# A two-layer decoder on one core: less work for GpSimd in a normalisation, another buffer for the sorted tiles' results, and another order

## The chip, the cores and the metric

The kernel runs on 1 core of one Trainium2 chip. The metric is the device time of one execution in microseconds. TensorE (PE; PEld is its weight load), VectorE (DVE), ScalarE (ACT), GpSimd (POOL) and SyncE (SP) each work through a queue of their own in the order in which the program was built; semaphores join them.

## The reference, cut to what matters

Sixteen sequences of 128 tokens with 256 features go through two decoder layers in float32. Every sub-layer is added to x after a normalisation of x:

```python
def _layernorm(x, axis=-1, eps=1e-05):
    m = jnp.mean(x, axis=axis, keepdims=True)
    v = jnp.var(x, axis=axis, keepdims=True)
    return (x - m) / jnp.sqrt(v + eps)
...
x = x + _L0_attn_ref(_layernorm(x), qk, ov)                    # causal, one head
x = x + _L0_xattn_ref(_layernorm(x), ctx, ctx, mask, ...)      # 16 heads of 16, over the context
x = x + _L0_ffn_ref(_layernorm(x), ...)                        # 16 blocks of 64, the best 4 by a router
x = x + _L1_attn_ref(_layernorm(x), ...)                       # 16 heads, and adds its own input
x = x + _L1_xattn_ref(_layernorm(x), ctx, ctx, cell, ...)      # windows of 64, rotary, four more norms
x = x + _L1_ffn_ref(_layernorm(x), ...)                        # 8 experts of 128, the best 2, and a shared one
```

The last one, for each token t, with `combine` zero for all but two of the eight experts e:

```python
hmid = jax.nn.silu(g) * u            # g, u = x @ w_gate[e].T, x @ w_up[e].T
y = jnp.einsum('tei,ehi->teh', hmid, w_down)
routed_out = jnp.einsum('te,teh->th', combine, y)
out = routed_out + shared_out
```

## The kernel before, in words

**Tiles.** Two sequences make a lane: x[l] is a tile of 128 tokens by 2 by 256, and eight lanes (NL) stay in the on-chip memory from start to end. Matrices are float32; masks, router choices and one-hot products are bfloat16.

**The order.** Every piece of work is a generator (a thread). A planner, the class `Turns`, holds an estimated free time for each engine, a cost for each instruction and a list of free buffers for each tag (`LIMITS`). At each `yield` a thread names the engine that it needs next and the buffers that it takes; `run` picks the thread that could start first by the estimate, ties by rank, and records its instructions up to the next `yield`. The recorded order is the order of every engine's queue on the chip; nothing is reordered there. `LEAD` prefers threads that take score banks (`s`), `RELEASE` is added to the time at which a buffer is given back, and `indexed` (L162) adds 2000 ns to the planned landing of a transfer by index. None of these numbers is an instruction; they act through the order alone.

**Lanes in flight.** `TURN` (L1422) is the list of lane and layer pairs in the order in which they begin, first six lanes of layer 0, then layer 1 of lane 0, layer 0 of lane 6 and so on. At most five are in flight.

**Layer 0** of a lane (`layer_0`): causal attention, attention over the context, block feed-forward; TensorE's groups are pj, pr, s, oT, hp (hidden) and y.

**Layer 1** of a lane (`layer_1`): self attention, windowed attention (which normalises four times: the context, x twice, the heads' output), then, for lanes 0 to 4, `routing`. An attention of one sequence computes its scores twice: once for the maximum (VectorE, `top`), and again with the maximum subtracted inside the product (GpSimd adds it to the queries, `qs`, and spreads the keys, `kb`).

**The experts.** Lanes 0 to 4 are sorted: `routing` scatters each normalised token to two rows of a table in device memory (`to_experts`, 20 transfers by index on GpSimd's queue). When all five are through, `plan` counts the tiles and 27 `expert_tile` threads each gather an expert's weights and 128 tokens (`we`, two transfers by index), multiply, and store 128 results to `by_experts` from ScalarE's queue. One buffer `p` of 1024 columns holds the weights in 768 and the tokens in 256; the results (`yo`) are copied over the tokens. After all tiles and the five `shared` threads, `combining` gathers 20 times from `by_experts` (`yg`) and adds to x. Lanes 5 to 7 are dense: `expert_ffn` computes all eight experts (gu, wb, y) with weights that are loaded after layer 0.

**The normalisation.** `normalise` (L392) has VectorE compute mean and variance (bn_stats and bn_aggr, `mv`). GpSimd then makes `rstd` in two instructions (add, power) and `less` = -mean x rstd in two more. One half of the tile is normalised by VectorE (`xn`, subtract and multiply), the other by ScalarE with `less` as bias and `rstd` as scale. It is called 77 times. GpSimd's instructions on 128 x 2 elements, the indexed transfers (L168) and everything else of GpSimd stand in one queue.

The class of routers (`ranks`, `chosen`): VectorE compares the scores (eq, gt), GpSimd combines them, VectorE counts, and TensorE transposes the choice (`ptt`).

Of the kernel before, what the change touches and what calls it, by code (L numbers as in the profile page):

```python
# [9 lines left out]
F32 = mybir.dt.float32  # L10
# [4 lines left out]
ALU = mybir.AluOpType  # L15
AX = mybir.AxisListType

B, S, D = 16, 128, 256
P = 128
# [62 lines left out]
class Turns:  # L82
# [3 lines left out]

    LEAD = 200.0
    HOP = 70.0  # L90
    HOP_FROM_PE = 200.0
    SWITCH = 91.0
    PART = 0.0
    RELEASE = 0.0

    def __init__(self, nc, limits):
        self.nc = nc
# [64 lines left out]
    def indexed(self, out, out_index, src, src_index):  # L162

        at = lambda i: None if i is None else bass.IndirectOffsetOnAxis(ap=i, axis=0)
        self.charge(POOL, 1050.0)
        self.moved(4 * int(np.prod((src if src_index is None else out).shape)))
        self.now.at += 2000.0
        self.nc.gpsimd.indirect_dma_start(out, at(out_index), src, at(src_index))  # L168

    def fetch(self, out, src):  # L170
# [102 lines left out]
def decoder(ctx: ExitStack, tc: tile.TileContext, a: dict, out: bass.AP):  # L273
# [118 lines left out]
    def normalise(src, free=False):  # L392

        yield DVE
        mv = small.tile([P, G, 2], F32, tag="mv", name="mv")
        for j in range(G):
            st = small.tile([P, 6], F32, tag="st", name="st")
            q.dve("bn_stats", st, src[:, j, :])
            q.dve("bn_aggr", mv[:, j, :], st)
        yield POOL  # L400
        rstd = small.tile([P, G], F32, tag="rstd", name="rstd")
        q.pool("tensor_scalar", rstd, mv[:, :, 1], EPS, None, ALU.add)
        q.pool("tensor_tensor", rstd, rstd, power, ALU.pow)

        less = small.tile([P, G], F32, tag="less", name="less")
        q.pool("tensor_tensor", less, mv[:, :, 0], rstd, ALU.mult)
        q.pool("tensor_scalar", less, less, -1.0, None, ALU.mult)
        yield DVE, dict(xn=1)
        xn = new("xn", [P, G, D], "xn")

        def one(j):
            if j:
                yield ACT
                q.act("activation", xn[:, j, :], src[:, j, :], AF.Identity, bias=less[:, j : j + 1], scale=rstd[:, j : j + 1])
            else:
                yield DVE
                q.dve("tensor_scalar", xn[:, j, :], src[:, j, :], mv[:, j, 0:1], rstd[:, j : j + 1], ALU.subtract, ALU.mult)

        yield [one(j) for j in range(G)]
        if free:  # L420
            q.give("xn")
        return xn
# [670 lines left out]
    def expert_tile(g, i):  # L1093

        yield POOL, dict(p=1)

        we = new("p", [P, HC, S], "we").rearrange("p h s -> p (h s)")
        xg = yo = we[:, 3 * D :]
        q.indexed(we[:, 0 : 3 * D], None, a["L1_experts"], g.tile_weights[:, i : i + 1])
        yield POOL  # L1100
        q.indexed(xg, None, g.to_experts, g.tile_rows[:, i : i + 1])
        yield PE, dict(bank=1)
        t = bank([P, DC, S], "xgt")
        for d in range(DC):
            q.transpose(t[:, d, :], xg[:, d * P : (d + 1) * P], ident)
        yield ACT, dict(xe=1)
        xgT = new("xe", [P, DC, S], "xgT")
        q.act("copy", xgT, t)
        q.give("bank")
        yield PE, dict(bank=1, tmp=1)  # L1110
        gu = bank([P, 2, P], "gu2")
        for d in range(DC):
            wt = we[:, d * D : (d + 1) * D].rearrange("p (n f) -> p n f", f=P)
            q.matmul(gu, xgT[:, d, :], wt, start=d == 0, stop=d == DC - 1)
        q.give("xe")
        yield ACT
        sg = new("tmp", [P, P], "sg2")
        q.act("activation", sg, gu[:, 0, :], AF.Tanh, scale=0.5)
        yield DVE, dict(p0=1)
        h = new("p0", [P, P], "h2")  # L1120
        q.dve("scalar_tensor_tensor", sg, sg, 1.0, gu[:, 0, :], ALU.add, ALU.mult)
        q.dve("scalar_tensor_tensor", h, sg, 0.5, gu[:, 1, :], ALU.mult, ALU.mult)
        q.give("tmp")
        q.give("bank")
        yield PE, dict(bank=1)
        t = bank([P, P], "hT2")
        q.transpose(t, h, ident)
        q.give("p0")
        yield ACT, dict(pT0=1)
        hT = new("pT0", [P, P], "hT")  # L1130
        q.act("copy", hT, t)
        q.give("bank")
        yield PE, dict(bank=1)
        y = bank([P, D], "y2")
        q.matmul(y, hT, we[:, DC * D : 3 * D], start=True, stop=True)
        q.give("pT0")
        yield ACT
        q.act("copy", yo, y)
        q.give("bank")
        q.load(g.by_experts[i * P : (i + 1) * P, :], yo, engine=ACT)  # L1140
        q.give("p")

    def combining(g, l):

# [262 lines left out]
    def layer_1(l):  # L1407
# [4 lines left out]
        if g is not None:  # L1412
            yield from routing(l)
            g.left -= 1
            at = q.now.at
            q.start(shared(l), 2 * NL + l, at)
            if g.left == 0:
                q.start(sorted_experts(g), 2 * NL + min(g.lanes), at)

    IN_FLIGHT = 5  # L1420

    TURN = [(0, l) for l in range(6)]  # L1422
    for l in range(NL):
        TURN += [(1, l), (0, l + 6)] if l + 6 < NL else [(1, l)]

    def more():
        n = begun[0]
# [119 lines left out]
```

## Time and profile before

| | |
|---|---|
| median of 3 runs (range) | 840.87 us (835.97 to 841.37) |
| the profiled execution, its span | 843.06 us, 841.3 us |
| granted TensorE clock, mean | 0.979 |
| busy: PE, PEld | 782.0 us (93%), 617.5 us (73%) |
| busy: DVE, ACT, POOL | 479.2 us (57%), 393.0 us (47%), 450.4 us (54%) |
| the chain that ended last, by engine | PE 76%, DVE 9%, POOL 5%, ACT 4% |
| POOL waited longest | rstd for mv of DVE, 88.8 us; qs for less of ACT, 60.9 us |
| transfers by index on POOL's queue | 27 + 27 gathers (we), 20 scatters (to_experts), 20 gathers (yg) |

A busy PE is not a PE at its peak, since the ends of matmuls are modelled. A group's row reads: line, engine, operation, out<-in, form, count, then busy us and mean ns of one, then the idle time of the engine ahead of it and what ended it. All instructions of one engine carry the planner's line (L135 matmuls, L144 VectorE, L149 ScalarE, L155 GpSimd, L168 transfers by index), so they are told apart by the names of their tiles.

### The profile page before, as it was taken

The page shows a single profiled execution, that of the slowest core. Times are in us where ns is not written, and L with a number is a line of the kernel's source. Part 1 is how long each engine was busy: PE and PEld are TensorE (multiplying, and loading weights), DVE is VectorE, ACT ScalarE, POOL GpSimd, SP SyncE. Part 2 cuts the span into 40 slices and gives each one's busy share as a digit, 9 for nine tenths or more (in the row PEclk, how much of TensorE's full clock was granted, in tenths as well). Part 3 has the DMA queues.
Part 4 walks back from the last instruction along what each step waited for, and adds up shares of the span by engine and source line. Part 5 has one row for each costly group of instructions (what it writes and reads, how often), then busy time and mean ns, then how long its engine had stood idle before and what let it go on. Part 6 is the DMA issues. An engine that isn't in the chain of part 4 may idle for free.

```text
span 841.3 us, 19812 instructions
## 1 busy us (share of the span) xinstructions
PE 782.0 (93%) x7886; PEld 617.5 (73%) x7886; DVE 479.2 (57%) x1257; ACT 393.0 (47%) x874; POOL 450.4 (54%) x720
## 2 busy tenths in 40 slices
PE   6999999999999999999999999999878699989984
PEld 5777678878778677777777777777656477877862
DVE  4455636546626537656785478578485553364263
ACT  4545355344355364646652755646545234333310
POOL 5325535514335266566776756966764843474053
PEclk9999899999999999999999999999999999999997
DMA  8457440601201011010013111101201533455133
GB/s 287 157 149 221 133 134 29 182 17 35 57 3 38 14 58 33 15 51 14 20 46 128 63 44 52 59 26 51 77 21 32 163 101 111 129 163 164 57 93 119
DMA packets 60940, 70.41 MB, mean 84 GB/s; under 512 B 8848, under 2 KB 52496, under 8 KB 60208
## 3 DMA queue, kind: packets, MB, share of 16 engines
q1 hardware_dynamic: 51584, 46.20, 17.7%
q0 software_dynamic: 5376, 19.40, 7.9%
q10 hardware_dynamic: 3888, 3.54, 1.2%
q8 instruction: 62, 1.02, 0.5%
q14 instruction: 30, 0.25, 0.1%
HBM read 43.96 MB, written 20.97 MB: 77 GB/s over the span
## 4 chain that ended last, share of the span: by engine, by line
PE 76%; DVE 9%; POOL 5%; ACT 4%; issue 3%; another core or an unknown queue 2%; DMA 0%; ACTq 0%; POOLq 0%; DVEq 0%
PE s L135 15%; PE y L135 11%; PE pj L135 11%; PE gu L135 8%; PE pr L135 8%; PE hp L135 8%; PE oT L135 5%; PE tps L140 3%; PE o L140 2%; ACT p L149 2%; DVE top L144 1%; PE rt L135 1%; DVE x L144 1%; POOL rstd L155 1%
## 5 line engine op out<-in xcount | busy, mean ns | idle before, releaser
L144 DVE TENSOR_REDUCE top<-s 128x8 f32<-128x1024 f32 x96 | 113.0, 1218 | 54.4 <-PE s L135 49.9
L149 ACT ACTIVATE p<-s 128x1024 f32<-128x1024 f32 x96 | 95.2, 1024 | 63.7 <-PE s L135 58.4
L155 POOL TENSOR_TENSOR qs<-qT,less 128x512 f32<-128x512 f32 x48 | 61.6, 1288 | 67.9 <-ACT less L149 60.9
L155 POOL TENSOR_SCALAR rstd<-mv 128x2 f32<-128x2 f32 x77 | 18.5, 241 | 95.1 <-DVE mv L144 88.8
L135 PE MATMUL s<-qs,kb 32*128 32x128 f32 x1536 | 62.1, 290 | 7.6 <-POOL qs L155 3.8
L135 PEld LDWEIGHTS s<-qs,kb 32*128 32x128 f32 x1536 | 51.8, 191 | 22.2 <-issue 7.0
L135 PE MATMUL hp<-srcT,L_w 128*128 128x256 f32 x256 | 67.6, 394 | 0.0
L135 PE MATMUL s<-kb,qT 32*128 32x256 f32 x768 | 61.7, 407 | 3.2 <-DVE top L144 3.0
L135 PE MATMUL y<-L_w,hm 128*128 128x256 f32 x256 | 58.8, 383 | 0.7 <-ACT gained L149 0.6
L155 POOL TENSOR_TENSOR rstd<-rstd,power 128x2 f32<-128x2 f32 x77 | 55.1, 716 | 6.4
L149 ACT ACTIVATE sg<-gu 128x256 f32<-128x256 f32 (+1 forms) x67 | 22.7, 341 | 73.8 <-PE gu L135 57.0
L155 POOL TENSOR_SCALAR kb<-kT,consts 128x256 f32<-128x256 f32 x96 | 53.4, 567 | 6.9 <-ACT kT L149 6.0
L149 ACT ACTIVATE hm<-hp,cols 128x256 f32<-128x256 f32 x64 | 26.8, 470 | 60.9 <-PE hp L135 60.8
L135 PE MATMUL oT<-p,v 128*32 128x128 f32 x1536 | 53.6, 281 | 1.3 <-ACT gained L149 0.9
L135 PEld LDWEIGHTS hp<-srcT,L_w 128*128 128x128 f32 x256 | 45.3, 195 | 12.2 <-issue 2.8
L168 POOL DMA_INDIRECT we<-in_L_experts,tile_weights x27 | 26.2, 971 | 52.2 <-DMA by_experts<-we 13.2
L135 PEld LDWEIGHTS y<-L_w,hm 128*128 128x128 f32 x256 | 47.7, 190 | 8.4 <-issue 1.1
L135 PEld LDWEIGHTS s<-kb,qT 32*128 32x128 f32 x768 | 38.3, 186 | 19.9 <-issue 8.6
L144 DVE SCALAR_TENSOR_TENSOR sg<-sg,gu 128x256 f32<-128x256 f32 (+1 forms) x67 | 24.3, 363 | 45.6 <-ACT sg L149 42.6
L135 PEld LDWEIGHTS oT<-p,v 128*32 128x32 f32 x1536 | 40.1, 112 | 12.6 <-issue 8.1
L135 PE MATMUL gu<-srcT,gu 128*128 128x256 f32 x192 | 47.5, 394 | 1.3 <-DVE hm L144 0.6
L144 DVE TENSOR_TENSOR x<-x,y 128x256 f32<-128x256 f32 x32 | 13.3, 417 | 61.3 <-PE y L135 50.5
(211 smaller groups left out, 1822.0 us busy)
## 6 DMA issues: line engine op xcount, KB each, us to landing
to_experts<-zero SPq DMA_DIRECT2D x7, 1280.0 KB
unseen<-hidden SPq DMA_DIRECT2D x128, 64.0 KB
c<-in_ctx SPq DMA_DIRECT2D x16, 256.0 KB
by_experts<-we ACTq DMA_DIRECT2D x27, 128.0 KB
x<-in_x SPq DMA_DIRECT2D x8, 256.0 KB
L_w<-in_L_w SPq DMA_DIRECT2D x2, 1024.0 KB
hidden<-plain SPq DMA_DIRECT2D x32, 64.0 KB
swap<-kT SPq DMA_DIRECT2D x16, 128.0 KB
```

The source lines that it names most:

```text
L135: self.nc.tensor.matmul(out, lhsT, rhs, **kw)
L140: self.nc.tensor.transpose(out, src, ident)
L144: getattr(self.nc.vector, name)(out, *args, **kw)
L149: getattr(self.nc.scalar, name)(out, *args, **kw)
L155: getattr(self.nc.gpsimd, name)(out, *args, **kw)
L168: self.nc.gpsimd.indirect_dma_start(out, at(out_index), src, at(src_index))
```

## The change

Four edits stand in the diff. In `normalise` the addition of EPS and `less` move from GpSimd to VectorE, `less` as one instruction; GpSimd keeps the power; mv, st, rstd and less get eight buffers each instead of four. In `expert_tile` the results go to a buffer of the tag xe (128 x 256, four of them, shared with xgT), and p is given back after the last matmul. In the planner, a transfer by index lands 1000 ns later by the estimate, LEAD is 100 and RELEASE 30. In the order of threads, layer 1 begins after five lanes of layer 0 and `shared` ranks behind all other expert work.

```diff
-    LEAD = 200.0
+    LEAD = 100.0
...
-    RELEASE = 0.0
+    RELEASE = 30.0
...
     def indexed(self, out, out_index, src, src_index):
...
-        self.now.at += 2000.0
+        self.now.at += 3000.0
...
     def normalise(src, free=False):
         yield DVE
-        mv = small.tile([P, G, 2], F32, tag="mv", name="mv")
+        mv = small.tile([P, G, 2], F32, tag="mv", name="mv", bufs=8)
         for j in range(G):
-            st = small.tile([P, 6], F32, tag="st", name="st")
+            st = small.tile([P, 6], F32, tag="st", name="st", bufs=8)
             q.dve("bn_stats", st, src[:, j, :])
             q.dve("bn_aggr", mv[:, j, :], st)
+        rstd = small.tile([P, G], F32, tag="rstd", name="rstd", bufs=8)
+        q.dve("tensor_scalar", rstd, mv[:, :, 1], EPS, None, ALU.add)
         yield POOL
-        rstd = small.tile([P, G], F32, tag="rstd", name="rstd")
-        q.pool("tensor_scalar", rstd, mv[:, :, 1], EPS, None, ALU.add)
         q.pool("tensor_tensor", rstd, rstd, power, ALU.pow)
-        less = small.tile([P, G], F32, tag="less", name="less")
-        q.pool("tensor_tensor", less, mv[:, :, 0], rstd, ALU.mult)
-        q.pool("tensor_scalar", less, less, -1.0, None, ALU.mult)
         yield DVE, dict(xn=1)
         xn = new("xn", [P, G, D], "xn")
+        less = small.tile([P, G], F32, tag="less", name="less", bufs=8)
+        q.dve("scalar_tensor_tensor", less, mv[:, :, 0], -1.0, rstd, ALU.mult, ALU.mult)
...
     def expert_tile(g, i):
...
-        xg = yo = we[:, 3 * D :]
+        xg = we[:, 3 * D :]
...
         q.matmul(y, hT, we[:, DC * D : 3 * D], start=True, stop=True)
         q.give("pT0")
-        yield ACT
+        q.give("p")
+        yield ACT, dict(xe=1)
+        yo = new("xe", [P, D], "yo")
         q.act("copy", yo, y)
         q.give("bank")
         q.load(g.by_experts[i * P : (i + 1) * P, :], yo, engine=ACT)
-        q.give("p")
+        q.give("xe")
...
     def layer_1(l):
...
-            q.start(shared(l), 2 * NL + l, at)
+            q.start(shared(l), 2 * NL + l + NL, at)
...
-    TURN = [(0, l) for l in range(6)]
+    TURN = [(0, l) for l in range(5)]
     for l in range(NL):
-        TURN += [(1, l), (0, l + 6)] if l + 6 < NL else [(1, l)]
+        TURN += [(1, l), (0, l + 5)] if l + 5 < NL else [(1, l)]
```

## The prediction

> **What bounds the kernel now.** I read the busy times first, then the stretches of the span, the chain of work that ended last, the groups of instructions and, where TensorE stood still, the timeline.
>
> ```profile
> PE 782.0 (93%) x7886; PEld 617.5 (73%) x7886; DVE 479.2 (57%) x1257; ACT 393.0 (47%) x874; POOL 450.4 (54%) x720
> 440.00:560.00 120.00, 116.04 (x1380) 91.97 (x1379) 76.06 (x195) 69.75 (x141) 82.56 (x138) 1.00 0.20 66
> 560.00:680.00 120.00, 100.19 (x1136) 76.61 (x1138) 77.86 (x220) 55.06 (x115) 79.28 (x121) 0.93 0.21 64
> 680.00:800.00 120.00, 115.19 (x757) 93.24 (x756) 54.16 (x163) 46.52 (x141) 48.43 (x58) 1.00 0.42 125
> 800.00:841.30 41.30, 26.05 (x104) 19.41 (x102) 21.20 (x65) 3.15 (x9) 19.06 (x20) 0.86 0.35 105
> ```
>
> The stretch rows give PE, weight load, DVE, ACT and POOL busy time, then the granted clock. TensorE is the bound, and its matmuls are the same before and after; only its standing still can change, 841.3 - 782.0 = 59.3 us. Of that 11.3 lie in the first 120 us (three rows of 40 us, not shown), 4.3 in 120 to 440 us, 4.0 in 440 to 560, 19.8 in 560 to 680, 4.8 in 680 to 800 and 15.3 in the tail. The last hidden-layer matmul of layer 0 ends at 447 us, so 560 to 680 is nearly pure attention of layer 1, then the start of the sorted tiles. What the change is worth is decided there and in the tail.
>
> **The change part by part.**
>
> *The normalisation.* GpSimd does four instructions on two elements, 77 times; the change leaves it the power.
>
> ```profile
> L155 POOL TENSOR_TENSOR rstd<-rstd,power 128x2 f32<-128x2 f32 x77 | 55.1, 716 | 6.4
> L155 POOL TENSOR_SCALAR less<-less 128x2 f32<-128x2 f32 x77 | 19.0, 247 | 6.8
> L155 POOL TENSOR_SCALAR rstd<-mv 128x2 f32<-128x2 f32 x77 | 18.5, 241 | 95.1 <-DVE mv L144 88.8
> L155 POOL TENSOR_TENSOR less<-mv,rstd 128x2 f32<-128x2 f32 x77 | 15.8, 206 | 6.0
> ```
>
> Removed from GpSimd: 19.0 + 18.5 + 15.8 = 53.3 us of 450.4. Added to VectorE: one addition and one two-input instruction, 77 times each. No row shows these two; the nearest are
>
> ```profile
> L144 DVE TENSOR_SCALAR den<-den x8: 169/338/418, 383.3 to 748.7; 128x2 f32<-128x2 f32 x8
> L144 DVE RECIPROCAL den<-den x8: 165/166/167, 383.7 to 749.1; 128x2 f32<-128x2 f32 x8
> L144 DVE SCALAR_TENSOR_TENSOR weight<-weight,den x5: 161/163/448, 383.9 to 614.7; 128x4 f32<-128x4 f32 x5
> ```
>
> (minimum, median, maximum in ns). The reciprocal of the same size never varies, the addition doubles when GpSimd is at work. Below, a pair costs 161 + 161 = 322 ns, above 338 + 415 = 753 ns (415 is the mean of the other two-input row, sel, on 128x16). I take 280 + 200 = 480 ns, nearer the lower end because GpSimd will be less busy: 77 x 0.48 = 37 us, so VectorE goes to some 516 us and GpSimd to 397.
>
> The Trainium skill, "SBUF — State Buffer", section "Who interferes with whom", speaks against this edit: VectorE's copies and scalar instructions may take a port pair that GpSimd owns too, and whichever starts second waits for the whole instruction. The 169 to 418 ns of den agree with it. By the rule alone each addition could stand behind a whole GpSimd instruction, 1.3 us for qs: the ten on the chain would cost 13 us instead of 2.8, and the sum below would be -6 instead of -16.
>
> What counts is the chain of waits. Ten of the 77 normalisations lie on it; one of them reads
>
> ```profile
> 547.90 0.19 DVE mv L144
> 548.10 0.08 issue
> 548.17 0.23 POOL rstd L155
> 548.40 0.07 issue
> 548.47 0.72 POOL rstd L155
> 549.19 0.07 issue
> 549.26 0.20 POOL less L155
> 549.46 0.08 issue
> 549.54 0.22 POOL less L155
> ```
>
> (start, length, what). The ten additions take 2.8 us on the chain, the less instructions 4.1, the gaps between them 10 x 0.22 = 2.2: 9.1 removed. Ten pairs on VectorE give back 10 x 0.48 = 4.8. So -4. Better than that: pairs of 0.322, and POOL's share of the chain (5%) of the 53.3 us freed, 2.7 more: -8.5. Worse: pairs of 0.753, and 58 us more VectorE work of which its chain share (9%) shows, 5.2: +3.6. The new waits in VectorE's queue: less waits for the power, mostly directly ahead of xn, which already waits for it; the addition waits for GpSimd's instruction of the moment, and behind it stand reductions of scores (top), for which TensorE's next transpose waits. That is the 5.2. The eight buffers instead of four cost nothing: no wait of VectorE in the list of waits is for a reader of mv, st or less.
>
> *The new order.* TURN, LEAD, RELEASE, the longer landing in indexed and the later rank of shared write another instruction order for all engines; I compared the orders of the two built programs. Three things stand out.
>
> First, a router's choice is no longer stuck. Now, in TensorE's longest single stop:
>
> ```profile
> 660.11 0.94 POOL L168 DMA_INDIRECT we<-in_L_experts,tile_weights  x1 [0.30 <-PE y L135]
> 663.85 0.95 POOL L168 DMA_INDIRECT we<-in_L_experts,tile_weights  x1 [0.30 <-issue]
> 666.04 0.41 POOL L155 TENSOR_TENSOR eq<-eq,consts 128x128 bf16<-128x128 bf16 x1
> 671.37 0.40 PE L135 MATMUL ptt<-ident,chosen 128*128 128x128 bf16 x2 [6.57 <-DVE chosen L144]
> ```
>
> Between the router's matmuls at 645.6 us and this eq, GpSimd's queue holds nine gathers. Afterwards the first gather stands behind eq and gt. The stop of 6.57 us goes, and the clock of 0.61 and 0.53 after it (668 to 676 us; the 4 us at 0.53 hold 1.9 us of loss): -8.5. But TensorE then has only two blocks of scores, about 5 us, between that router and its ptt, and VectorE's instructions between sc and chosen (one pair of top reductions, 2 x 1.22 us, a normalisation of 2 x 0.41 + 2 x 0.18 + 0.48 + 0.42, and some sixteen small ones of about 0.2) sum to 7.7 us, GpSimd's eq and gt to 0.8 more: a new stop of 3. Net -5.5, between -8.5 and 0.
>
> Second, layer 1 starts one sequence pair earlier (five pairs of layer 0 ahead of it, not six), so 14 attention score blocks instead of 18 are left after the last hidden-layer matmul, and none overlaps the sorted tiles (now two). From 440 to 680 us TensorE stands still 23.8 us; without the 6.57 that is 17.2 for 18 blocks, 0.96 each. Four blocks fewer in the thin stretch: -4, between -8 (twice that, if the blocks that go are the worst) and 0 (they stand as still elsewhere).
>
> Third, the tail. After the last sorted tile 8 dense gate/up blocks are left, not 7, so the results are ready one block of 8 matmuls (1.73 us on the chain) earlier. The 20 gathers behind them stay as they are, 1.25 us apart:
>
> ```profile
> 804.76 0.95 POOL L168 DMA_INDIRECT yg<-by_experts,results  x1 [25.30 <-DVE results L144]
> ```
>
> They run to 829.6 and the span ends 11.7 us later; -1.7, at worst 0. The SP queue keeps its kinds of transfers; loads and swaps change places by a few, and its waits hardly reach TensorE, which shows one 0.8 us wait for a transfer.
>
> *The buffer of yo.* The weight buffer p goes back when the last matmul has read it, not when the store has landed. GpSimd's gathers now wait 13.5 us for stores and 7.8 for the copy, 21.3 us in the trace, but only 5.7 us of gathers are on the chain and TensorE is 96% busy there: -1, at best -5.7. The cost side: yo and xgT share four xe buffers, so ScalarE can now wait for a store (issued 676.97, released its waiter at 679.52: 2.5 us) with everything behind it. At 3.9 us per tile (105 us over 27) four buffers cover two tiles, so I take none; if every fifth tile waited 2.5 us it would be +12.
>
> *The sum.* -4 - 5.5 - 4 - 1.7 - 1 = -16.2. The profiled execution took 843.06 us (1.8 outside its span); that gives 826.9. The median of the runs shown is 840.87, 2.2 lower, so I name 825. All best ends: -8.5 - 8.5 - 8 - 1.7 - 5.7 = -32.4, 808; all worst: +3.6 + 0 + 0 + 0 + 12 = +15.6, 856.
>
> **The rivals.**
>
> *VectorE becomes the bound of the attention stretch (slower).* Place: 560 to 660 us, where VectorE is already busy 77.9 of 120 us, and 9.46 of 10 in 620 to 630. Layer 1 with its routing has six normalisations per pair, and the 48 attention blocks with their 113 us of reductions are now packed into a shorter part of the span. Price: 48 x 0.753 = 36 us in VectorE's queue, less the 9.1 taken off the chain, +27, on top of which only the tail's -1.7 is kept: 866 at full exposure; at half (18 - 9.1 - 1.7 = +7) it is 848, the point from which it decides. I name two thirds, 24 - 9.1 - 1.7 = +13, 854. Against it: before 560 us VectorE is 56% busy and TensorE hardly waits.
>
> *The order gives nothing (no change).* The two gains of the order, 9.5, come back as stops elsewhere, since every queue was rewritten: -6.7, 834. For it: the new ptt stop; against it: the nine gathers are plainly gone from ahead of eq.
>
> *The stores block ScalarE.* +12 in place of -1 and the rest as forecast: 838, no change; were the order's gains to fail too, 847.
>
> **How the numbers follow.** Forecast 825: 0.52. VectorE-bound, 854: 0.26. Order gives nothing, 834: 0.14. Stores, 838: 0.08. About 1% is what a measurement here tells from no change (the runs shown span 0.6%). Faster 0.52; within 1% the two middle cases less the part of the stores' case that ends slower, 0.18; slower 0.30. The forecast's own range is 808 to 832; with the others 808 to 858, which leaves out less than the last quarter of VectorE's case and as much below.
>
> **What would show it.** Right: POOL busy near 397 and DVE near 516; no ptt wait over 4 us in the stretch of the sorted tiles; PE idle in the 120 us ahead of them down from 20 to about 10; yg gathers starting about 787 to 790 us. Wrong: DVE over 9 tenths in several slices with PE waiting for top or xn (the first rival), waits of ACT for by_experts stores (the third), or the same PE idle sum in other places (the second).

## The result, and the profile after

The changed kernel takes 844.44 us (median of 11 runs, 843.41 to 847.72) beside 838.99 us for the kernel before (median of 11, 835.28 to 841.56). The ratio is 1.0058, 95% interval 1.0033 to 1.0082: 0.6% slower, by the ratio 4.9 us. The forecast, 825 us, lay 16 us below the 840.87 us of the table before. The profiled execution took 844.61 us with a span of 842.8 us and a mean granted clock of 0.972 (before 843.06, 841.3 and 0.979).

First the busy line of the page, then the stretches of the span (columns: PE, weight load, DVE, ACT and POOL busy, granted clock, DMA share, GB/s):

```profile
PE 781.7 (93%) x7886; PEld 618.2 (73%) x7886; DVE 507.4 (60%) x1411; ACT 392.6 (47%) x874; POOL 398.0 (47%) x489
440.00:560.00 120.00, 115.77 (x1318) 91.44 (x1317) 78.68 (x216) 67.89 (x138) 57.68 (x70) 0.96 0.17 54
560.00:680.00 120.00, 99.96 (x1268) 73.25 (x1267) 88.76 (x237) 54.57 (x109) 64.43 (x73) 0.90 0.13 42
680.00:800.00 120.00, 115.38 (x650) 95.61 (x648) 55.62 (x179) 46.34 (x143) 57.51 (x64) 1.00 0.48 149
800.00:843.00 43.00, 28.23 (x131) 23.04 (x129) 23.21 (x70) 5.40 (x15) 19.03 (x20) 0.89 0.35 107
```

GpSimd lost 52.4 us of work as meant and VectorE gained 28.2. TensorE is as busy as before, and from 560 to 680 us it stands still 20.0 us, as before (19.8); from 120 to 440 us it stands still 8.7 us instead of 4.3, in the first 120 us 9.0 instead of 11.3. The granted clock in 440 to 560 and 560 to 680 us fell from 1.00 and 0.93 to 0.96 and 0.90.

What ended TensorE's waits (in all, times, longest, us), first in the kernel before, then in the changed one:

```profile
PE tps L140 <- DVE xn L144: 8.7, 5, 6.2
PE ptt L135 <- DVE chosen L144: 6.6, 1, 6.6
...
PE s L135 <- DVE top L144: 3.0, 4, 1.1
```

```profile
PE tps L140 <- DVE xn L144: 11.2, 3, 6.1
PE s L135 <- DVE top L144: 7.7, 8, 3.3
PE s L135 <- POOL eq L155: 3.4, 1, 3.4
...
PE s L135 <- DVE less L144: 2.1, 1, 2.1
...
PE ptt L135 <- DVE chosen L144: 0.7, 2, 0.5
```

The longest wait for xn is in both that of the first transpose, 6 us from the start. The stop of 6.57 us for ptt is gone. In its place stand stops in the attention stretch: 4.91 us for xn, 3.33 for top, 3.36 for eq. The timeline shows how the first of them came about (start, length, engine, instruction, idle time before it and its releaser):

```profile
605.02 0.80 DVE L144 TENSOR_SCALAR rstd<-mv 128x2 f32<-128x2 f32 x1
605.07 0.72 POOL L155 TENSOR_TENSOR x<-x,rows 128x256 f32<-128x256 f32 x1
...
606.56 1.26 POOL L155 TENSOR_TENSOR qT<-qT,consts 128x512 f32<-128x512 f32 x1
606.68 1.16 DVE L144 SCALAR_TENSOR_TENSOR less<-mv,rstd 128x2 f32<-128x2 f32 x1
607.76 0.40 DVE L144 TENSOR_SCALAR xn<-c,mv,rstd 128x256 f32<-128x256 f32 x1
...
608.31 1.12 PE L140 MATMUL tps<-consts,xn 128*128 128x128 f32 x4 [4.91 <-DVE xn L144]
```

The addition takes 0.80 us and less 1.16 us, where their medians are 0.170 and 0.155, and by the trace each ends within 0.03 us of the GpSimd instruction that was at work. But VectorE's queue from 603 to 608 us also holds the statistics of a second normalisation and three other instructions ahead of that less: the order put the one that TensorE waited for last.

Where the kernel's stages lie, from the instructions of three tiles (count: duration ns min/median/max, first and last start):

```profile
L135 PE MATMUL hp<-srcT,L_w x256: 379/379/635, 97.2 to 496.1; 128*128 128x256 f32 x128
L135 PE MATMUL gu<-we,xgT x108: 379/379/483, 694.5 to 798.4; 128*128 128x256 f32 x108
L168 POOL DMA_INDIRECT yg<-by_experts,results x20: 942/946/1079, 809.5 to 833.3; - x20
```

Before, the last hidden-layer matmul of layer 0 started at 446.3 us, the sorted tiles' matmuls ran from 662.9 to 794.1, and the yg gathers from 804.8. Layer 0 now ends 50 us later, since layer 1 began earlier.

For all that follows a span is split in three: idle (the span less PE's busy time); clock loss (busy time times one minus the granted clock, summed over rows of 4 us); and the rest, the work at full clock. For before: 59.3 + 12.4 + 769.6 us; for after: 61.1 + 15.4 + 766.2. The span grew by 1.5 us: 1.8 more idle, 3.0 more clock loss and 3.4 less work, up to rounding. These are single executions, and they hold only 1.5 of the 4.9 us. The eleven executions of after agree with a larger clock loss: their granted clock has a median of 0.972, that of before in the five sets of runs beside the experiments 0.975 to 0.978.

### The profile page after: what moved, and what is told of

Same layout as the page of the kernel before. It is cut to its first block, busy times and chain, and to the rows that moved or that the text cites. A ratio compares the mean times of both kernels' runs of the same rounds, so it can differ in the third digit from the quotient of the medians.

```text
span 842.8 us, 19656 instructions
## 1 busy us (share of the span) xinstructions
PE 781.7 (93%) x7886; PEld 618.2 (73%) x7886; DVE 507.4 (60%) x1411; ACT 392.6 (47%) x874; POOL 398.0 (47%) x489
## 5 line engine op out<-in xcount | busy, mean ns | idle before, releaser
L149 ACT ACTIVATE p<-s 128x1024 f32<-128x1024 f32 x96 | 95.4, 1025 | 57.1 <-PE s L135 56.5
L135 PE MATMUL s<-qs,kb 32*128 32x128 f32 x1536 | 64.1, 293 | 11.9 <-DVE top L144 4.4
L135 PEld LDWEIGHTS hp<-srcT,L_w 128*128 128x128 f32 x256 | 45.0, 194 | 11.3 <-issue 3.7
L135 PEld LDWEIGHTS s<-kb,qT 32*128 32x128 f32 x768 | 38.3, 192 | 20.3 <-issue 10.7
L140 PE MATMUL tps<-consts,xn 128*128 128x128 f32 x244 | 39.1, 286 | 13.2 <-DVE xn L144 11.2
L149 ACT ACTIVATE less<-topT,consts 128x128 f32<-128x128 f32 x96 | 29.6, 370 | 38.7 <-PE topT L140 36.1
L144 DVE BATCH_NORM_STATS2 st<-x 128x6 f32<-128x256 f32 x106 | 43.2, 408 | 4.6 <-DMA x<-in_x 3.6
```

The lines of the kernel that those rows point to most:

```text
L135: self.nc.tensor.matmul(out, lhsT, rhs, **kw)
L140: self.nc.tensor.transpose(out, src, ident)
L144: getattr(self.nc.vector, name)(out, *args, **kw)
L149: getattr(self.nc.scalar, name)(out, *args, **kw)
```

## The experiments

"Order kept" means that the instruction is recorded directly on the engine while the planner is charged as before, so that no other instruction changes its place in a queue. The traces show it: but for the instructions that an edit names, TensorE, VectorE, ScalarE and GpSimd have the same sequence as in the kernel whose order is kept. "Planned anew" means that the planner wrote all queues. Ratios are to the kernel before on the same chip, with 95% intervals.

| run | ratio, interval | span | idle | clock loss |
|---|---|---|---|---|
| before | 1 | 841.3 | 59.3 | 12.4 |
| after | 1.0058 (1.0033 to 1.0082) | 842.8 | 61.1 | 15.4 |
| *order kept* | | | | |
| e1 new normalisation | 0.9956 (0.9923 to 0.9990) | 836.0 | 56.4 | 10.6 |
| e3 its VectorE pair twice | 1.0196 (1.0150 to 1.0242) | 854.8 | 69.7 | 12.1 |
| e5 choice ahead of gathers | 0.9971 (0.9953 to 0.9989) | 842.0 | 57.4 | 13.1 |
| e6 GpSimd's part removed only | 0.9919 (0.9896 to 0.9942) | 837.4 | 55.0 | 13.2 |
| e7 only less moved | 0.9949 (0.9927 to 0.9972) | 840.6 | 60.3 | 9.7 |
| e11 yo in its own buffer | 0.9950 (0.9913 to 0.9988) | 832.1 | 58.5 | 6.4 |
| e12 normalisation and choice | 0.9941 (0.9906 to 0.9976) | 834.1 | 54.0 | 10.9 |
| e13 normalisation and yo | 0.9971 (0.9955 to 0.9986) | 843.5 | 54.5 | 18.0 |
| e14 all three | 0.9971 (0.9954 to 0.9988) | 839.9 | 57.1 | 11.2 |
| *order of after kept* | | | | |
| e2 after with the old normalisation | 1.0091 (1.0059 to 1.0122) | 847.6 | 65.8 | 14.2 |
| *planned anew* | | | | |
| e4 HOP 75 | 1.0061 (1.0034 to 1.0088) | 846.2 | 67.8 | 10.3 |
| e16 RELEASE 10 | 1.0117 (1.0089 to 1.0146) | 858.5 | 65.5 | 23.6 |
| e18 LEAD 180 | 0.9997 (0.9969 to 1.0024) | 841.0 | 60.6 | 10.6 |
| e8 TURN five | 1.0459 (1.0435 to 1.0483) | 881.3 | 82.5 | 29.5 |
| e9 after with TURN six | 1.0040 (1.0007 to 1.0072) | 840.3 | 58.4 | 16.3 |
| e10 LEAD, RELEASE, landing, rank | 1.0345 (1.0285 to 1.0405) | 866.0 | 78.7 | 18.6 |
| e15 new normalisation | 1.0325 (1.0295 to 1.0354) | 873.7 | 76.1 | 18.0 |
| e17 landing and rank | 1.0127 (1.0090 to 1.0165) | 854.1 | 77.0 | 11.2 |

The span and its parts are those of one profiled execution, which can lie several us from the median; the ratio decides. Judged by the intervals, two ratios near 1 can be told apart when they differ by some 0.4% (3.4 us) or more.

### The instructions without the order: e1, e2, e3

```diff
+        rstd = small.tile([P, G], F32, tag="rstd", name="rstd", bufs=8)
+        nc.vector.tensor_scalar(rstd, mv[:, :, 1], EPS, None, ALU.add)
         yield POOL
-        q.pool("tensor_scalar", rstd, mv[:, :, 1], EPS, None, ALU.add)
+        q.charge(POOL, 200 + 1.42 * 2)
         q.pool("tensor_tensor", rstd, rstd, power, ALU.pow)
-        q.pool("tensor_tensor", less, mv[:, :, 0], rstd, ALU.mult)
-        q.pool("tensor_scalar", less, less, -1.0, None, ALU.mult)
+        q.charge(POOL, 200 + 2.15 * 2)
+        q.charge(POOL, 200 + 1.42 * 2)
         yield DVE, dict(xn=1)
+        nc.vector.scalar_tensor_tensor(less, mv[:, :, 0], -1.0, rstd, ALU.mult, ALU.mult)
```

> The new normalisation in the order of the kernel before: the addition and less are recorded on VectorE where the new code has them, but the planner is charged as for the four GpSimd instructions, so that no other instruction changes its place. It separates what the instructions cost from what the new order costs. Theory A (the order is what lost the time): GpSimd falls from 450 to about 398 us busy, VectorE rises from 479 to about 507, and the time falls by the 4 us that the sum had, ratio 0.993 to 0.999 (833 to 838 beside 839). Theory B (VectorE's two instructions cost more than GpSimd's three gave): the kernel is as slow as the changed one or slower, ratio 1.005 or more, 843 upwards, with TensorE waiting longer for xn and top than the 8.7 and 3.0 us of before.

Measured 0.9956: theory A. The busy line of its page and two of TensorE's waits:

```profile
PE 779.6 (93%) x7886; PEld 616.4 (74%) x7886; DVE 508.8 (61%) x1411; ACT 393.1 (47%) x874; POOL 397.9 (48%) x489
```

```profile
PE tps L140 <- DVE xn L144: 8.0, 4, 6.2
...
PE s L135 <- DVE top L144: 2.9, 5, 1.1
```

VectorE and GpSimd are as busy as in the changed kernel, yet TensorE waits no longer for xn and top than before (8.7 and 3.0). The 11.2 and 7.7 us of the changed kernel are not a price of these instructions alone. The stop for ptt stays, with 5.8 us: less work for GpSimd does not by itself bring the choice forward.

The mirror, in the changed kernel:

```diff
-        q.dve("tensor_scalar", rstd, mv[:, :, 1], EPS, None, ALU.add)
+        q.charge(DVE, 150 + 1.05 * 2)
         yield POOL
+        nc.gpsimd.tensor_scalar(rstd, mv[:, :, 1], EPS, None, ALU.add)
         q.pool("tensor_tensor", rstd, rstd, power, ALU.pow)
+        nc.gpsimd.tensor_tensor(less, mv[:, :, 0], rstd, ALU.mult)
+        nc.gpsimd.tensor_scalar(less, less, -1.0, None, ALU.mult)
         yield DVE, dict(xn=1)
-        q.dve("scalar_tensor_tensor", less, mv[:, :, 0], -1.0, rstd, ALU.mult, ALU.mult)
+        q.charge(DVE, 150 + 1.05 * 2)
```

> The mirror: the changed kernel's order with the normalisation of before. GpSimd again does the addition and both instructions of less, VectorE neither; the planner is charged as in the changed kernel, so that all other instructions keep its places. Theory A: the time rises by some 4 us above the changed kernel's 844, to 847 to 851, ratio to before 1.009 to 1.014, GpSimd near 450 us busy. Theory B: it falls below the changed kernel, to 838 or less, ratio 1.000 or below, and TensorE's longest stop for xn, 4.9 us at 608 us, is gone.

Measured 1.0091, at the foot of theory A's range: 0.3% slower than the changed kernel, which the intervals don't tell from no difference, but clearly slower than before, although the old normalisation is back. Its waits of TensorE for top and xn, and three of its stops, read

```profile
PE s L135 <- DVE top L144: 10.3, 10, 3.3
PE tps L140 <- DVE xn L144: 10.2, 2, 6.3
```

```profile
607.82 0.30 PE L140 MATMUL tps<-consts,xn 128*128 128x128 f32 x1 [3.85 <-DVE xn L144]
641.94 0.70 PE L135 MATMUL s<-kb,qT 32*128 32x256 f32 x4 [3.33 <-DVE top L144]
648.24 2.09 PE L135 MATMUL s<-qs,kb 32*128 32x128 f32 x32 [2.12 <-POOL qs L155]
```

In the changed kernel TensorE stands still 4.91, 3.33 and 2.12 us at the same three places (608, 640 and 647 us). So the new instructions make the first stop 1.1 us longer, and the rest belongs to the order. What is slow in the changed kernel is therefore its order, or the results' buffer, which e2 keeps as well; e11 below finds a buffer of their own for the results faster and not slower, though with two buffers and not the four that xgT shares.

The third kernel writes each of the two VectorE lines twice:

```diff
         nc.vector.tensor_scalar(rstd, mv[:, :, 1], EPS, None, ALU.add)
+        nc.vector.tensor_scalar(rstd, mv[:, :, 1], EPS, None, ALU.add)
...
         nc.vector.scalar_tensor_tensor(less, mv[:, :, 0], -1.0, rstd, ALU.mult, ALU.mult)
+        nc.vector.scalar_tensor_tensor(less, mv[:, :, 0], -1.0, rstd, ALU.mult, ALU.mult)
```

> As the first of these kernels, but VectorE does each of the two new instructions twice (the second writes the same values again). 154 more VectorE instructions, some 28 us more VectorE time if each costs what the first did. It measures the price of VectorE time at these places. Theory A: VectorE near 535 us busy and 3 to 5 us more than the first kernel, since ten normalisations lie on the chain at 0.36 each. Theory B: 10 us or more above the first kernel.

Measured 857.8 us, 20 more than e1 (837.8), against A's 3 to 5. VectorE rose by 34.5 us to 543.3, TensorE's idle time by 13.3. VectorE time at these places is not free; the first pair is cheap because it takes the place of something. The next two runs measure that.

### What the pair costs, and what the relief gives: e6, e7

```diff
-        nc.vector.tensor_scalar(rstd, mv[:, :, 1], EPS, None, ALU.add)
...
-        q.pool("tensor_tensor", rstd, rstd, power, ALU.pow)
+        q.pool("tensor_tensor", rstd, mv[:, :, 1], power, ALU.pow)
...
-        nc.vector.scalar_tensor_tensor(less, mv[:, :, 0], -1.0, rstd, ALU.mult, ALU.mult)
...
-  bias=less[:, j : j + 1]
+  bias=mv[:, j, 0:1]
```

(against e1)

> Order kept; GpSimd does only the power, and VectorE gets nothing for it: the addition of EPS is left out, and ScalarE takes the mean as its bias in place of less. It measures what the relief of GpSimd is worth by itself. By the prediction's chain term, 9.1 us (ratio 0.989). By the third kernel, in which a further pair of VectorE instructions cost 20 us, the pair of the first kernel hides a relief of up to 24 us: ratio 0.972 to 0.980.

Measured 0.9919 (0.9896 to 0.9942), 6.8 us less than before: nearer the chain term's 0.989, which the interval just leaves out, than what e3 suggested. (ScalarE reads mv here, and rstd is the power of mv alone; the instructions left are the same.) So the relief of GpSimd gives 6.8 us (4.9 to 8.8) and the pair takes back 0.9956 - 0.9919 = 0.37%, 3.1 us, with an interval from about nothing to 6.6. A second pair (e3) cost 20 us, at least three times as much: the price of VectorE time isn't linear here. Why it bends, these runs don't settle.

In e7 the addition goes back to GpSimd (against e1):

```diff
-        nc.vector.tensor_scalar(rstd, mv[:, :, 1], EPS, None, ALU.add)
         yield POOL
-        q.charge(POOL, 200 + 1.42 * 2)
+        q.pool("tensor_scalar", rstd, mv[:, :, 1], EPS, None, ALU.add)
```

> Half of the normalisation edit, order kept: the addition of EPS stays on GpSimd, and only less goes to VectorE, as one instruction. The addition costs GpSimd 0.24 us and a gap of 0.08 in the chain, VectorE 0.17 with no gap behind its own mv. If the length of the chain decides, this is 1 to 2 us slower than the first kernel (839, ratio 0.997). If VectorE's queue decides, as the third kernel suggests, it is 3 to 8 us faster than the first one (830 to 835, ratio 0.987 to 0.993).

Measured 0.9949 (0.9927 to 0.9972), not to be told from e1's 0.9956, and between the two expectations, whose nearer ends lie in its interval: this run doesn't decide between them. Moving less alone is worth as much as moving both: one VectorE instruction (median 0.16 us, mean 0.34) for two of 0.21 and 0.25 us (means) in GpSimd's queue. Where the addition is done makes no difference that these runs can show.

### The choice and the gathers: e5, e12

```diff
         q.dve("tensor_tensor", gt, other, own, ALU.is_gt)
+        if n == NE:
+            nc.gpsimd.tensor_tensor(eq, eq, tri.unsqueeze(1).to_broadcast(shape), ALU.mult)
+            nc.gpsimd.tensor_tensor(gt, gt, eq, ALU.add)
         yield POOL
-        q.pool("tensor_tensor", eq, eq, tri.unsqueeze(1).to_broadcast(shape), ALU.mult)
-        q.pool("tensor_tensor", gt, gt, eq, ALU.add)
+        ...   # charged for both if n == NE, else as before
```

> The kernel before, with its order, but for one thing: the two GpSimd instructions of an expert router's choice (eq, gt) are recorded directly behind VectorE's two comparisons, so that in GpSimd's queue they stand ahead of the gathers that held up the choice. It tests the prediction's second term alone, without a new plan. Prediction's theory: the stop of 6.57 us for ptt shrinks below 1 us and 5 to 8 us of the time go with it, ratio 0.990 to 0.994 (833). Rival, that a stop which is taken away comes back a little later, because VectorE, GpSimd and ScalarE still have the same work before the sorted tiles: the ptt stop shrinks, the time stays within 2 us of before, and TensorE's idle time from 560 to 680 us stays near 20 us.

Measured 0.9971 (0.9953 to 0.9989): 2.4 us, less than half of the prediction's 5.5. From 560 to 680 us TensorE stands still 18.0 us, so the rival is nearer. TensorE's timeline says where the rest went:

```profile
663.02 0.41 PE L140 MATMUL xgt<-consts,we 128*128 128x128 f32 x2 [1.66 <-DMA we<-to_experts,tile_rows]
663.26 1.89 PE L135 MATMUL gu<-we,xgT 128*128 128x256 f32 x8
664.99 0.27 PE L135 MATMUL ptt<-ident,chosen 128*128 128x128 bf16 x2
...
668.53 0.41 PE L140 MATMUL xgt<-consts,we 128*128 128x128 f32 x2 [2.84 <-DMA we<-to_experts,tile_rows]
```

ptt runs without a wait, and TensorE then stands still 1.66 + 2.84 = 4.5 us for the tokens of the sorted tiles, which before landed while it stood at ptt (it waited 0.79 us for them in all). The stop had covered part of the wait for the gathers.

> The first and the fifth of these kernels in one: new normalisation and the choice ahead of the gathers, the order otherwise that of before. If their gains (0.9956 and 0.9971) lie on different parts of the span they add: ratio 0.9927, 836.5 beside 842.5. If freeing GpSimd already brought the choice forward, the choice adds nothing: 0.9956.

e12 holds the diffs of e1 and e5. Measured 0.9941 (0.9906 to 0.9976), between the two expectations; the interval holds both.

### The results' buffer: e11

```diff
-        xg = yo = we[:, 3 * D :]
+        xg = we[:, 3 * D :]
...
         yield ACT
+        yo = work.tile([P, D], F32, tag="yo", name="yo", bufs=2)
         q.act("copy", yo, y)
```

> The kernel before with its order, in which the results of a sorted tile go to two buffers of their own, so that a gather into p no longer waits for the store but only for the last matmul. The waits of gathers for stores (13.5 us) go; by the prediction's term -1, ratio 0.998 to 1.000. Rival: +12, stores that hold up ScalarE (two buffers are fewer than the changed kernel's four, so this is the harder test): ratio 1.01, with waits of ScalarE for by_experts of some 2.5 us each.

Measured 0.9950 (0.9913 to 0.9988): 4.2 us, more than the term of 1. What the gathers waited for in GpSimd's queue:

```profile
POOL we L168 <- PE hT L140: 16.1, 8, 6.4
...
POOL we L168 <- PE y L135: 3.5, 3, 2.4
```

The waits for stores (13.5 us) and for the copy (7.8) are gone, and waits of much the same sum for TensorE stand there: 19.6 for 21.3. ScalarE waits for a store once, 0.5 us, so the rival is out. TensorE's idle time fell by only 0.8 us in this profile and the clock loss by 6.0; but the profiled execution is the fastest of the twelve (833.90 us, median 836.20), so where the gain lies stays open.

### Both, and all three: e13, e14

e13 holds the diffs of e1 (without bufs=8, so with four small buffers) and of e11; e14 that of e5 as well.

> Both edits of instructions and nothing of the order: the new normalisation (with four small buffers each, as in the kernel before) and yo in two buffers of its own, planner charged as before. If the two gains add, 0.9956 x 0.995 = 0.9906, 832.5 beside 840.5; the changed kernel's order then costs 1.0058 / 0.9906 = 1.5%, 13 us. If they overlap (both free GpSimd's queue ahead of gathers), 0.995 as each by itself, and the order costs 1.1%.

> As the one before it, with the experts' choice ahead of the gathers as well. The choice was worth 0.3% alone and 0.15% on top of the new normalisation: 0.989 if it adds, the same as its neighbour if the earlier gathers already take its place. The fastest version that the runs point to.

Both measured 0.9971. The gains don't add: 0.9906 lies outside e13's interval of 0.9955 to 0.9986, and so, barely, does the 0.995 of gains that overlap. The choice adds nothing on top (e14 is as its neighbour). The profile of e13:

```profile
PE 788.9 (94%) x7886; PEld 622.6 (74%) x7886; DVE 508.0 (60%) x1411; ACT 392.7 (47%) x874; POOL 397.9 (47%) x489
```

TensorE stands still only 54.5 us, 4.8 less than before, but is busy 6.9 us longer with the same 7886 matmuls: the clock loss is 18.0 us instead of 12.4. Much of that belongs to this execution: it is the slowest of e13's twelve (845.28 us at a mean granted clock of 0.972; the medians are 840.89 and 0.979, and before has 0.978 there). The intervals of e1, e11 and e13 overlap between 0.9955 and 0.9986, so each edit by itself, and both together, may be worth the same 0.14% to 0.45%. Whether one gain takes the place of the other, or four small buffers cost something against eight, the runs don't tell apart. What is settled is the sign: with the old order the instructions of the change are faster than before, in its own order slower; what was not run in the old order is the four buffers that the results share with xgT. By e13 the order costs 1.0058 / 0.9971 = 1.0087, some 7 us.

### Plans made anew: e8, e9, e10, e15, e17

```diff
-    TURN = [(0, l) for l in range(6)]
+    TURN = [(0, l) for l in range(5)]
...
-        TURN += [(1, l), (0, l + 6)] if l + 6 < NL else [(1, l)]
+        TURN += [(1, l), (0, l + 5)] if l + 5 < NL else [(1, l)]
```

> The kernel before with only the list of lanes changed: layer 1 begins after five lanes of layer 0 and not six, the order planned anew. The prediction's third term: fewer attention blocks in the thin stretch, 4 us faster (ratio 0.995), between 8 and 0. Rival: a new plan lands anywhere between 0.995 and 1.010, and TensorE's idle time from 440 to 680 us doesn't fall below the 23.8 us of before.

Measured 1.0459, 39 us slower, outside both expectations. The busy line of its page, the hidden-layer matmuls and two of TensorE's waits:

```profile
PE 798.8 (91%) x7886; PEld 626.8 (71%) x7886; DVE 481.1 (55%) x1257; ACT 391.3 (44%) x874; POOL 447.5 (51%) x720
```

```profile
L135 PE MATMUL hp<-srcT,L_w x256: 379/379/792, 97.2 to 520.6; 128*128 128x256 f32 x128
```

```profile
PE s L135 <- DVE top L144: 11.7, 13, 3.6
...
PE gu L135 <- DVE hm L144: 7.8, 2, 7.3
```

Of the 40.0 us that the span grew, 23.2 are idle time and 17.1 clock loss: a busy TensorE that runs slower between many stops. Layer 0 ends at 521 us.

e9 takes that edit alone out of the changed kernel:

```diff
-    TURN = [(0, l) for l in range(5)]
+    TURN = [(0, l) for l in range(6)]
...
-        TURN += [(1, l), (0, l + 5)] if l + 5 < NL else [(1, l)]
+        TURN += [(1, l), (0, l + 6)] if l + 6 < NL else [(1, l)]
```

> The changed kernel with one edit undone: layer 1 begins after six lanes of layer 0 again, planned anew. Beginning after five, alone, cost 39 us in the eighth kernel, so in the changed kernel either TURN is what loses and the other edits hide most of it, or TURN and the planner's numbers only work together. Theory A (TURN loses by itself): 825 to 838, ratio 0.980 to 0.995, with the last hidden-layer matmul of layer 0 near 447 us again, not 496. Theory B (each plan is a draw of its own): anywhere between 0.995 and 1.045.

Measured 1.0040 (1.0007 to 1.0072), theory B: 39 us in one plan, and in another 1.5 us (1.0058 against 1.0040), which the intervals don't tell from nothing. The last hidden-layer matmul is back at 448 us, and the ptt stop is back, with 7.7 us. TURN has no fixed price of its own.

e10 makes the planner's four edits and nothing else, e17 only the last two of them:

```diff
-    LEAD = 200.0
+    LEAD = 100.0        # e10 only
-    RELEASE = 0.0
+    RELEASE = 30.0      # e10 only
...
-        self.now.at += 2000.0
+        self.now.at += 3000.0
...
-            q.start(shared(l), 2 * NL + l, at)
+            q.start(shared(l), 2 * NL + l + NL, at)
```

> The kernel before with only the planner's numbers changed (LEAD 100, RELEASE 30, an indexed transfer landing 1 us later by the estimate) and shared ranked last; TURN, the normalisation and yo as before. Theory A: these are what holds the changed kernel's order together, and with six lanes ahead they gain, ratio 0.985 to 0.997, without the 6.57 us stop for ptt. Theory B: a draw of its own, 0.995 to 1.03.

Measured 1.0345: theory B, a little above its end.

> The kernel before with only the two numbers that act late: a transfer by index lands 1 us later by the estimate, and shared is ranked last. Up to the first scatter of a routing (near 380 us) the order must be that of before, and TensorE's idle time from 120 to 380 us too. Prediction's theory: gathers and shared work later in the order free the choice and the tail, ratio 0.990 to 0.998, without the 6.57 us stop. Rival (a new plan is a draw): 1.003 to 1.03, the loss all behind 380 us.

Measured 1.0127, the rival. TensorE's idle time from 120 to 440 us is 3.6 us (before 4.3), so the early part is as it was; from 560 us on it stands still 55.0 us instead of 39.8, most of the increase from 800 us on (26.1, before 15.2).

e15 makes only the normalisation edit of the change, through the planner:

```diff
+        q.dve("tensor_scalar", rstd, mv[:, :, 1], EPS, None, ALU.add)
         yield POOL
-        q.pool("tensor_scalar", rstd, mv[:, :, 1], EPS, None, ALU.add)
         q.pool("tensor_tensor", rstd, rstd, power, ALU.pow)
-        q.pool("tensor_tensor", less, mv[:, :, 0], rstd, ALU.mult)
-        q.pool("tensor_scalar", less, less, -1.0, None, ALU.mult)
         yield DVE, dict(xn=1)
+        q.dve("scalar_tensor_tensor", less, mv[:, :, 0], -1.0, rstd, ALU.mult, ALU.mult)
```

> The normalisation of the changed kernel alone, with the planner knowing of it, so that all queues are written anew. Its instructions are worth 0.9956 with the order kept. If a plan that knows the true costs is a better plan: below 0.9956. If any new plan is a draw beside a good one: 1.000 to 1.035, as the five new plans so far (1.004 to 1.046).

Measured 1.0325, the draw. e1 holds the same instructions and measures 0.9956; between the two lies the order alone, 3.7% or 32 us. From 120 to 440 us TensorE stands still 18.1 us, with e1's order 6.2.

### Shuffles without aim: e4, e16, e18

```diff
-    HOP = 70.0
+    HOP = 75.0        # e4
-    RELEASE = 0.0
+    RELEASE = 10.0    # e16
-    LEAD = 200.0
+    LEAD = 180.0      # e18
```

> Only the planner's cost of a hand-over between engines is changed, from 70 to 75 ns; no instruction is added or taken away, and the kernel before is otherwise untouched. It shows how far the time moves when the order alone is shuffled without any aim. Theory A (a new order moves stops about): the ratio differs from 1 by as much as the changed kernel's did, 0.3% to 1.5% in either direction, with the stops of TensorE at other places. The rival, that an order differs only where it is made to: within 0.2% of before.

> A second aimless shuffle: RELEASE 10 in place of 0, nothing else. If new orders scatter evenly about the old one, as likely below 1 as above; if the old order is a good draw, above 1.003 like the first shuffle (1.0061).

> A third shuffle without aim: LEAD 180 in place of 200, nothing else. If the old order is a good draw among many, above 1.003 like the other two (1.0061 and 1.0117); if those two were chance, as likely below 1.

Measured 1.0061, 1.0117 and 0.9997: e4 as its theory A has it, and two of the three above 1.003. Five nanoseconds in an estimate cost as much as the whole change. In e4 the stop is the same kind as the old one, a router's choice behind other work, but three times as long and in the tail:

```profile
812.86 0.39 PE L135 MATMUL ptt<-ident,chosen 128*128 128x128 bf16 x2 [18.50 <-DVE chosen L144]
```

With the changed kernel, nine plans were made anew; they lie between 0.9997 and 1.0459, none measurably below 1. In e18 the stop for ptt is gone without any aim (1.3 us of such waits), TensorE stands still 11.7 us from 560 to 680 us instead of 19.8, and behind 800 us 21.6 instead of 15.2: what went there came back here, and the time is that of before. The edits of the change give no sign of moving this scatter to the better.

## Why the prediction was wrong, and where it was right

**TensorE is the bound: right; "only its standing still can change": wrong.** In most of the runs the work at full clock is 765 to 772 us (773.0 in e3, 779.6 in e15). But the clock loss, which the sums left inside the busy time, goes from 6.4 to 29.5 us. Between the two profiled executions of before and after it is the larger part of what was lost: +3.0 beside +1.8 idle. The prediction counted clock loss only for the stop it wanted to remove (1.9 us).

**The normalisation, -4: right.** e1 gives 0.44%, -3.7 (0.8 to 6.5). The relief was put somewhat too high, 9.1 against 6.8 measured (e6, 4.9 to 8.8); the 4.8 given back is not told from the 3.1 measured. GpSimd's 397 us came out as 398.0, VectorE's 516 as 507.4. A pair is not cheaper than the 0.48 us forecast, though. Its rows in the changed kernel:

```profile
L144 DVE SCALAR_TENSOR_TENSOR less<-mv,rstd 128x2 f32<-128x2 f32 x77 | 23.8, 309 | 13.1 <-POOL rstd L155 13.0
L144 DVE TENSOR_SCALAR rstd<-mv 128x2 f32<-128x2 f32 x77 | 19.4, 252 | 2.7
```

That is 0.309 + 0.252 = 0.56 us a pair. VectorE's busy time rose by 28.2 us and not by 19.4 + 23.8 = 43.2: all its other instructions together last 8.5 us less than before, and records of neighbouring instructions overlap, which the busy time counts once.

The rule that spoke against it (the Trainium skill, "SBUF — State Buffer", section "Who interferes with whom") is at work, as the 605 to 608 us above show. In the changed kernel 29 of the 154 new instructions exceed their median by more than 0.08 us, all 29 end within 0.04 us of the end of a GpSimd instruction, and the excess sums to 18.0 us: 6.2 for the additions, 11.8 for less. The prediction weighed the rule for the additions only; the same section says that a VectorE instruction with two inputs from SBUF contends with GpSimd's reads, and less is such an instruction. By the rule alone the ten additions on the chain were put at 13 us; the whole pair costs 3.1 us. Most instructions escape: 101 of the 154 overlap no GpSimd instruction in the trace, and of the 53 that do, 24 are not longer for it, so here the rule doesn't hold for every meeting.

**The choice behind nine gathers, -5.5: the step failed in "Net -5.5".** The stop does go (0.7 us of ptt waits are left), but taken away by itself it gives 2.4 us. The prediction looked for the next wait in the router's own work and not among the sorted tiles whose tokens were still under way: 4.5 us of waits for gathers stand in its place (0.8 before).

**Layer 1 one pair earlier, -4: this is the step that failed.** "0.96 each" took the stops of the thin stretch as a price per score block, so that fewer blocks behind layer 0 meant fewer stops. From the last hidden-layer matmul to the first sorted tile TensorE stands still 16.2 us before (448 to 660 us, 18 blocks, 0.9 each) and 21.2 after (496 to 692 us, 14 blocks, 1.5 each). Alone the edit costs 39 us. In these runs stops follow the order in which the queues meet, and not the number of blocks. The same step fails for all three terms of the order: together they were put at -5.5 - 4 - 1.7 = -11.2 and at worst at 0, and the order of the changed kernel costs some +7 us (e13). New stops of a new plan were put at nothing, but for the one of 3 us behind the router.

**The tail, -1.7: not as forecast.** From the first yg gather to the end it is 33.3 us instead of 36.5, but that part was to stay as it is, and the gathers were to begin earlier. They begin 11.1 us behind the last start of gu in the sorted tiles (798.4 to 809.5), before 10.7; what is shorter is the time behind the last gather's start, 9.5 us instead of 12.6, for which the working had no reason. And 809.5 is not between 787 and 790, since everything ahead is later.

**The buffer p, -1 (to -5.7): undersized at most.** e11 measures -4.2 by itself (1.0 to 7.3), inside the range's far end, though little of it is left beside the normalisation. (The working's 3.9 us per tile is not what the rows of before give: 131.2 us from the first tile's gu to the last's, 4.9 for each of 27. In the changed kernel it is 103.9 us, 3.8 each.)

**The rivals.** VectorE as the bound (854): no. The changed kernel's top and xn waits look like it, with VectorE at 88.8 of 120 us from 560 to 680, but e1 shows the same VectorE load (508.8 us in all, 84.1 in that stretch) without those waits, and e2 the waits without the load (474.4). Two figures of that rival were misread and change nothing: the 77.9 us belong to 560 to 680 us, and VectorE is 58% busy before 560 us, not 56%. Stores that block ScalarE (838): no such wait in after, one of 0.5 us in e11. "The order gives nothing" (834) was the nearest, and named the reason, "every queue was rewritten"; what failed is its price. It took nothing as the worst that a new order can do. The runs show 0 to 39 us. The working had terms only for stops that it could see in the old profile, and those can only go; the new ones are in no row of before.

## What to carry to other kernels

When a planner writes the order, an edit has two prices: the instructions, which can be measured with the order pinned (charge the planner as before, record the new instructions in place), and the new plan, which is a draw. Measure that scatter with a few aimless shuffles before believing or rejecting an edit; here it was -0.0% to +1.2% for shuffles and up to +4.6% for edits, and pinned versions (e1, e7, e11, e12, at 0.994 to 0.996, and e13 and e14 at 0.997) beat both kernels. Before a stop is counted as gain, look for what else lands while it lasts: its gain ends where the next latest arrival begins.

## What the runs showed of the hardware that was not expected

- A VectorE instruction on 128 x 2 elements takes 0.144 to 1.23 us (less) and 0.169 to 1.48 us (the addition) in the same kernel, all 29 long ones ending within 0.04 us of a GpSimd instruction. Meeting one is not enough: 24 others overlap a GpSimd instruction and are not longer.
- The same matmuls are busy 773.6 us in e11 and 788.9 in e13, 15 us apart; the one profiled execution is the fastest of its twelve, the other the slowest. In the first 120 us the clock loss is 3.4 us in before and 0.0 in e11, although the instructions there are the same: a scatter between executions that no edit made. It shows in the times, too: among 29 executions of before on one chip the granted clock goes from 0.985 to 0.969 and the span from 833.8 to 845.5 us.
- The plan with the most idle time also has the largest clock loss (82.5 us idle, 29.5 clock loss in e8), but the two don't go in proportion: 77.0 us idle go with 11.2 in e17.
